# Attention scores of four graphs in one run on TensorE instead of two runs of two, in a two-layer graph attention kernel

## The chip, the cores and the metric

The kernel runs on one core of one Trainium2 chip. The metric is the device time in microseconds (us) of one execution, outputs compared with the reference. Before the change: 3203.19 us, median of three runs (3202.78 to 3203.3). Ratios are the mean time of one kernel's runs over that of the other's of the same rounds, so not quite the ratio of the medians that are quoted.

In the profile, PE is TensorE, PEld its weight loads, DVE is VectorE, ACT ScalarE, POOL GpSimd. A name like p1v is the PSUM bank p1 while it serves the matrix v; s is a bank of scores, av of the mix of values, e the exponentials, aT the normalised rows, transposed.

## The reference, cut to what matters

128 graphs of 128 nodes with 512 features, two layers, eight heads of 64, all in fp32. Layer 1 has an output matrix and a layer norm besides.

```python
scores = einsum('bihd,bjhd->bhij', Q, K) / sqrt(64)         # per graph and head: 128 x 128
scores = scores + (bias + log(adjacency + EPS))              # layer 1: log(clip(adj, 1e-8))
out    = einsum('bhij,bjhd->bihd', softmax(scores), V)
x      = out.reshape(...) + x                                # layer 0
x      = layer_norm(x + out.reshape(...) @ Wo.T + bo)        # layer 1
```

## The kernel before: what the change and the argument touch

Four graphs form a group; t counts the 64 groups of both layers (NG = 32, layer 1 from t = NG on). Each group has matrices v, q, k, and in layer 1 o. Each is a Strassen product P1 to P7 over seven slots; in many of them P2 (and P4 late on) is split again into four phases with small 128-column products. The functions of a slot are issued in program order on each engine.

```python
HALVES = slice(0, P // 2), slice(P // 2, P)

def matmul(dst, lhsT, rhs, start, stop):          # products: the array in two column halves
    for half in HALVES:
        nc.tensor.matmul(dst[half], lhsT[:, half], rhs, start=start, stop=stop, skip_group_check=True)

def scores(t, k):                                 # one visit: graphs 2k, 2k+1; the array in two row halves
    L, _ = split(t)
    s = {}
    for b in (2 * k, 2 * k + 1):
        s[b] = ps.tile([P, 2, KC, N], F32, tag="s", name=f"s_{t}_{b}", bufs=2)    # two banks a graph
        for c in range(KC):
            for r in range(2):
                ...
                nc.tensor.matmul(s[b][:, r, c], KT[t, k][at], QT[t, k][at], start=True, stop=True)
    for b, p in s.items():
        e = E[t, b] = work.tile([P, 2 * KC, N], F32, tag="e", name=f"e_{t}_{b}", bufs=2)
        nc.scalar.activation(e, p.rearrange("p r c j -> p (r c) j"), AF.Exp, scale=SCALE, ...)

def weigh(t, b):                                  # e *= adjacency, on VectorE
    ...
def mix(t, graphs):                               # e times V, again in column halves; its banks are "s" too
    ...
def move(t, k, engines):                          # 16 DMAs a pair: normalised rows to aT, in blocks of 32
    if k == 0:
        AT[t] = act.tile([P, G, KC, N], F32, tag="aT", name=f"aT_{t}")
    d = AT[t][:, 2 * k : 2 * k + 2].rearrange("p b c (t f) -> p (b c) t f", f=S)
    v = OR[t, k].rearrange("p b (c r) d -> p (b c) r d", r=2)
    for i in range(Q):
        for q in range(Q):
            src = v[i * S : (i + 1) * S, :, q // 2, (q % 2) * S : (q % 2 + 1) * S]
            engines[(i * Q + q) % len(engines)].dma_start(d[q * S : (q + 1) * S, :, i], src)
```

VectorE then transposes aT in place (turn) and the o matrix reads it. The eight PSUM banks are taken: four by the two buffers of s, and p0 to p3 by the products (p1 is P2's, p0 and p3 alternate from matrix to matrix). The two visits of a group stood at slots a + 4 and a + 11 (layer 1: a + 5 and a + 11), where a is the first slot behind k.

## Time and profile before

| | before |
|---|---|
| time, median | 3203.19 us |
| span of the profiled run | 3199.6 us |
| TensorE busy / share of the chain that ended last | 99% / 98% |
| VectorE, GpSimd, ScalarE busy | 68%, 63%, 33% |
| visits to the scores | 128 |
| TensorE's listed waits, all kinds | 8.5 us |

TensorE sets the time.

### The profile page before, as it was taken

The page shows a single profiled execution, that of the slowest core. Times are in us where ns is not written, and L with a number is a line of the kernel's source. Part 1 is how long each engine was busy: PE and PEld are TensorE (multiplying, and loading weights), DVE is VectorE, ACT ScalarE, POOL GpSimd, SP SyncE. Part 2 cuts the span into 40 slices and gives each one's busy share as a digit, 9 for nine tenths or more (in the row PEclk, how much of TensorE's full clock was granted, in tenths as well). Part 3 has the DMA queues.
Part 4 walks back from the last instruction along what each step waited for, and adds up shares of the span by engine and source line. Part 5 has one row for each costly group of instructions (what it writes and reads, how often), then busy time and mean ns, then how long its engine had stood idle before and what let it go on. Part 6 is the DMA issues. An engine that isn't in the chain of part 4 may idle for free.

```text
span 3199.6 us, 99332 instructions
## 1 busy us (share of the span) xinstructions
PE 3178.8 (99%) x41454; PEld 2454.4 (77%) x41454; DVE 2165.9 (68%) x4643; ACT 1043.3 (33%) x1763; POOL 2018.3 (63%) x2337
## 2 busy tenths in 40 slices
PE   9999999999999999999999999999999999999998
PEld 7777777777777777777887787878787777878785
DVE  6666666666666666676766666766666666766666
ACT  3333333333333333332323233323333233323332
POOL 4444433444433444468887878787787878787776
PEclk9999999999999999999999999999999999999999
DMA  5333333333333333342433434343433434343432
GB/s 126 84 80 82 79 80 75 84 81 82 79 75 80 84 81 81 94 110 54 82 87 76 95 73 98 68 95 72 83 85 76 94 74 97 72 100 65 92 77 77
DMA packets 1017266, 266.10 MB, mean 83 GB/s; under 512 B 942704, under 2 KB 949872, under 8 KB 1016816
## 3 DMA queue, kind: packets, MB, share of 16 engines
q1 hardware_dynamic: 1015152, 257.34, 36.2%
q8 instruction: 332, 5.44, 0.7%
q10 hardware_dynamic: 1408, 2.10, 0.2%
q14 instruction: 118, 0.97, 0.1%
q0 software_dynamic: 256, 0.26, 0.1%
HBM read 159.92 MB, written 67.11 MB: 71 GB/s over the span
## 4 chain that ended last, share of the span: by engine, by line
PE 98%; DVE 1%; POOL 0%; DMA 0%; issue 0%; ACT 0%; SPq 0%; DVEq 0%; POOLq 0%
PE p3v L135 10%; PE p3k L135 10%; PE p0q L135 10%; PE s L135 8%; PE av L135 7%; PE p2v L135 7%; PE p2q L135 7%; PE p2k L135 7%; PE p0o L135 7%; PE p0k L135 4%; PE p0v L135 4%; PE p3q L135 4%; PE p2o L135 3%; PE p1v L135 3%; PE p1k L135 3%; PE p1q L135 3%
## 5 line engine op out<-in xcount | busy, mean ns | idle before, releaser
L135 POOL TENSOR_TENSOR xn<-o,xn 128x512 f32<-128x512 f32 x128 | 149.0, 1186 | 653.6 <-DVE o L135 646.1
L135 DVE TENSOR_TENSOR e<-e,adjT 128x1024 f32<-128x1024 f32 x256 | 416.3, 1666 | 152.9 <-ACT e L135 152.9
L135 POOL TENSOR_TENSOR xn<-xn,row 128x512 f32<-128x512 f32 x256 | 356.3, 1414 | 128.6 <-DVE gw L135 120.5
L135 POOL TENSOR_TENSOR h<-h,xn 128x512 f32<-128x512 f32 x124 | 157.4, 1291 | 181.1 <-DVE h L135 181.1
L135 PE MATMUL av<-v,e 128*64 128x65 f32 x8192 | 262.4, 221 | 1.5 <-DVE e L135 1.5
L135 PE MATMUL s<-qT,kT 64*128 64x128 f32 x4096 | 263.1, 278 | 0.0
L135 PEld LDWEIGHTS av<-v,e 128*64 128x64 f32 x8192 | 258.0, 137 | 2.1 <-DVE e L135 2.1
L135 PEld LDWEIGHTS s<-qT,kT 64*128 64x128 f32 x4096 | 238.6, 188 | 22.2 <-issue 16.7
L135 PE MATMUL p3v<-wv,T 128*64 128x256 f32 (+1 forms) x2132 | 249.7, 361 | 2.5 <-DVE u3v L135 2.5
L135 PE MATMUL p3k<-T,wk 128*64 128x256 f32 (+1 forms) x2132 | 239.7, 360 | 0.0
L135 PE MATMUL p0q<-T,wq 128*64 128x256 f32 (+1 forms) x2132 | 239.7, 360 | 0.0
L135 ACT COPY o<-av 128x520 f32<-128x520 f32 x256 | 151.7, 593 | 168.1 <-PE av L135 159.3
L135 PEld LDWEIGHTS p3v<-wv,T 128*64 128x64 f32 x2132 | 163.3, 137 | 51.4 <-DVE u3v L135 2.9
L135 POOL TENSOR_TENSOR T<-xT 128x512 f32<-128x512 f32 x128 | 194.0, 1515 | 9.7 <-DVE xT L135 9.6
L135 DVE SCALAR_TENSOR_TENSOR gw<-xn,gw 128x512 f32<-128x512 f32 x256 | 196.5, 767 | 4.4
L135 POOL TENSOR_TENSOR h<-h,gamma 128x512 f32<-128x512 f32 x121 | 181.4, 1499 | 27.9 <-ACT h L135 27.9
L135 PEld LDWEIGHTS p3k<-T,wk 128*64 128x64 f32 x2132 | 149.0, 137 | 57.8
L135 PEld LDWEIGHTS p0q<-T,wq 128*64 128x64 f32 x2132 | 148.6, 137 | 58.1
L135 DVE STREAM_TRANSPOSE xT<-xT 128x512 f32<-128x512 f32 x252 | 176.9, 702 | 0.5 <-issue 0.5
L135 ACT ACTIVATE e<-s 128x1024 f32<-128x1024 f32 x128 | 124.3, 1023 | 124.9 <-PE s L135 124.9
L135 PE MATMUL p0o<-wo,T_o 128*64 128x256 f32 (+1 forms) x1368 | 161.1, 353 | 0.8 <-DVE u3o L135 0.4
L135 POOL TENSOR_TENSOR h<-h,beta 128x512 f32<-128x512 f32 x121 | 155.8, 1287 | 9.5
(271 smaller groups left out, 7146.0 us busy)
## 6 DMA issues: line engine op xcount, KB each, us to landing
x1d<-xn SPq DMA_DIRECT2D x64, 512.0 KB, 3.0
xT<-x1d SPq DMA_DIRECT2D x512, 64.0 KB, 2.5
xn<-x1d SPq DMA_DIRECT2D x64, 512.0 KB, 4.8
xT<-in_x_dram SPq DMA_DIRECT2D x496, 64.0 KB, 2.6
xn<-in_x_dram SPq DMA_DIRECT2D x62, 512.0 KB, 4.3
aT<-o SPq DMA_DIRECT2D x984, 32.0 KB, 2.0
out_dram<-h SPq DMA_DIRECT2D x60, 512.0 KB, 4.0
adjT<-in_adj_dram SPq DMA_DIRECT2D x256, 64.0 KB, 3.6
```

The source lines that it names most:

```text
L135: return lambda *args, **kw: self.tc.keep_in_program_order(f(*args, **kw))
```

## The change

Its intent is to cut the visits to the scores from two to one a group. The third graph has no s buffer, so it takes two banks of the products for a while (p1, and p0 or p3, whichever the matrix at hand doesn't use). As four graphs' exponentials now live at once, those of the first two go into buffers named h or xT. P2's phases, the weighings, moves, turns and row additions go to slots where those banks are free. In layer 1 from t > NG on, graphs 2,3 now come before 0,1. The core of the diff:

```diff
-    def scores(t, k):
+    def scores(t, graphs, spare=None):
...
-        for b in (2 * k, 2 * k + 1):
-            s[b] = ps.tile([P, 2, KC, N], F32, tag="s", name=f"s_{t}_{b}", bufs=2)
+        for i, b in enumerate(graphs):
+            k = b // 2
+            if i == 2:
+                s[b] = [ps.tile([P, KC, N], F32, tag=tag, name=f"s_{t}_{b}_{tag}") for tag in spare]
+            else:
+                p = ps.tile([P, 2, KC, N], F32, tag="s", name=f"s_{t}_{b}", bufs=2)
+                s[b] = [p[:, 0], p[:, 1], p]
...
+    EARLY = (0, 2, 3, 5)                    # slots of P2's four phases, now per matrix
+    for (which, t), n in at.items():
...
+        else:
+            phases = dict(v=(4, 5, 7, 9), q=(3, 4, 5, 7), k=(2, 3, 4, 5), o=(5, 7, 9, 10))[which]
...
-        step = 5 if t == NG else 7
-        for k in range(2 if t + 1 < LAST else 0):
-            put(pre, a + 4 + L * (1 - k) + step * k, scores, t, k)
...
+            visit, weighed, mixed, graphs = (
+                (3, (3, 3, 4, 5), (5, 7), (0, 1, 2, 3)), (3, (3, 3, 4, 5), (5, 7), (0, 1, 2, 3)), (5, (5, 5, 5, 7), (7, 9), (2, 3, 0, 1)),
+            )[(t >= NG) + (t > NG)]
+            put(pre, a + visit, scores, t, graphs, ("p1", "p0" if a // 7 % 2 else "p3"))
...
+                    put(post, m + (3, 1)[i], move, t, k, ...)
...
+                graphs = (2, 3, 0, 1) if t > NG else (0, 1, 2, 3)
+                put(post, first_pair, lambda t, bs: [turn(AT[t][:, b]) for b in bs], t, graphs[:2])
```

More of the change, by code (lines that the diff above doesn't have):

```diff
@@ L53 @@
     A11, A12, S4, NA22, S1, S2, S3 = range(7)
-    SLOTS = (
-        ("P1", "P4.1 b", "P2.1"), ("P4 b",), ("P3 b", "P4.2 b", "P2.2"), ("P6", "P4.3 b", "P2.3"), ("P5", "P4.4 b"),
-        ("P7", "P2.4"), (),
-    )
+    SLOTS = (("P1", "P4.1 b"), ("P4 b",), ("P3 b", "P4.2 b"), ("P6", "P4.3 b"), ("P5", "P4.4 b"), ("P7",), ())
     OPERANDS = {
@@ L169, in fast_path @@
     ps = ctx.enter_context(tc.tile_pool(name="ps", bufs=1, space=PSUM))
+    XTB = [act.tile([P, G, KC, N], F32, name=f"xT_{i}") for i in range(2)]
     X1D = [dram.tile([G, N, D], F32, name=f"x1d_{g}") for g in range(NG)]
@@ L184, in load_tiles @@
     def load_tiles(t):
-        XT[t] = act.tile([P, G, KC, N], F32, tag="xT", name=f"xT_{t}", bufs=2)
+        XT[t] = XTB[t % 2]
         AD[t] = act.tile([P, G, N], F32, tag="adjT", name=f"adjT_{t}", bufs=2)
@@ L343, in inner @@
             if phase == "1":
-                if i == "P2":
-                    out_tile()
                 t[i] = bank("p1") if i == "P2" else t["a"]
@@ L361, in inner @@
                 add(m, 0, p, v, 1, 3)
-                if i == "P2":
-                    add(1, 1, t["b"], t["u3"])
         def unit(i):
@@ L370, in unit @@
                 if (i, *phase) == ("P2", "1"):
-                    out_tile()
                     t["c"] = bank("p1")
@@ L377, in unit @@
                 return
+            if i == "C22":
+                return add(1, 1, t["b"], t["u3"])
             if i == "P1":
                 t["W"], t["B"] = W(), Bs()
+                out_tile()
                 t["a"] = bank("p3" if n % 2 else "p0")
@@ L390, in unit @@
                 kept("u3", p, 1, 1)
-                if "P2" not in inside:
-                    add(1, 1, t["b"], t["u3"])
             elif i == "P4":
@@ L458, in scores @@
                     at = half, c // 2, slice((c % 2 * 2 + b % 2) * N, (c % 2 * 2 + b % 2 + 1) * N)
-                    nc.tensor.matmul(s[b][:, r, c], KT[t, k][at], QT[t, k][at], start=True, stop=True)
-        for b, p in s.items():
-            e = E[t, b] = work.tile([P, 2 * KC, N], F32, tag="e", name=f"e_{t}_{b}", bufs=2)
-            nc.scalar.activation(
-                e, p.rearrange("p r c j -> p (r c) j"), AF.Exp, scale=SCALE,
-                **({"bias": C[t][:, 1, b : b + 1]} if L == 0 else {}),
-            )
+                    nc.tensor.matmul(s[b][r][:, c], KT[t, k][at], QT[t, k][at], start=True, stop=True)
+            if i > 1 or len(graphs) == 2:
+                E[t, b] = work.tile([P, 2 * KC, N], F32, tag="e", name=f"e_{t}_{b}", bufs=2)
+            elif t <= NG:
+                E[t, b] = work.tile([P, 2 * KC, N], F32, tag="h", name=f"e_{t}_{b}", bufs=2)
+            else:
+                E[t, b] = XT[t][:, 2 * i : 2 * i + 2].rearrange("p b c n -> p (b c) n")
+            e = E[t, b]
+            pieces = [(e[:, :KC], s[b][0]), (e[:, KC:], s[b][1])]
+            if i != 2:
+                pieces = [(e, s[b][2].rearrange("p r c j -> p (r c) j"))]
+            for e, p in pieces:
+                nc.scalar.activation(
+                    e, p, AF.Exp, scale=SCALE, **({"bias": C[t][:, 1, b : b + 1]} if L == 0 else {})
+                )
     def weigh(t, b):
@@ L494, in normalise @@
         o = OR[t, k]
-        if k == 0:
+        if t not in RC:
             RC[t] = small.tile([P, G, 2, KC], F32, tag="rc", name=f"rc_{t}", bufs=2)
@@ L527, in move @@
     def move(t, k, engines):
-        if k == 0:
+        if t not in AT:
             AT[t] = act.tile([P, G, KC, N], F32, tag="aT", name=f"aT_{t}")
@@ L674, in fast_path @@
             row_.append([(mats[j], i) for j, i in units if 0 <= j < len(mats)])
+    EARLY = (0, 2, 3, 5)
+    for (which, t), n in at.items():
+        if t < NG:
+            phases = EARLY if t == 0 else dict(v=(3, 4, 5, 7), q=(1, 2, 3, 5), k=EARLY)[which]
+        elif t == NG or (which, t) == ("v", NG + 1):
+            phases = dict(v=(3, 4, 5, 7), q=(1,), k=(0,), o=EARLY)[which]
+        elif (which, t) == ("o", LAST - 2):
+            phases = (3, 4, 5, 7)
+        else:
+            phases = dict(v=(4, 5, 7, 9), q=(3, 4, 5, 7), k=(2, 3, 4, 5), o=(5, 7, 9, 10))[which]
+        if (which, t) == ("o", NG):
+            phases = (0,)
+        for i, slot_ in enumerate(phases):
+            row_[7 * n + slot_].append((mats[n], f"P2.{i + 1}"))
+        row_[7 * n + 5].append((mats[n], "C22"))
     def slot(which, t, i):
@@ L689, in fast_path @@
         a = slot("k", t, 7)
-        step = 5 if t == NG else 7
-        for k in range(2 if t + 1 < LAST else 0):
-            put(pre, a + 4 + L * (1 - k) + step * k, scores, t, k)
-            for b in (2 * k, 2 * k + 1):
-                put(pre, a + 4 + L * (1 - k) + step * k, weigh, t, b)
-            if t + 1 < LAST:
-                m = a + 7 + L * (1 - k) + step * k
+        if t + 1 < LAST:
+            visit, weighed, mixed, graphs = (
+                (3, (3, 3, 4, 5), (5, 7), (0, 1, 2, 3)), (3, (3, 3, 4, 5), (5, 7), (0, 1, 2, 3)), (5, (5, 5, 5, 7), (7, 9), (2, 3, 0, 1)),
+            )[(t >= NG) + (t > NG)]
+            put(pre, a + visit, scores, t, graphs, ("p1", "p0" if a // 7 % 2 else "p3"))
+            for i, b in enumerate(graphs):
+                put(pre, a + weighed[i], weigh, t, b)
+            for i in range(2):
+                m, k = a + mixed[i], graphs[2 * i] // 2
                 put(pre, m, mix, t, (2 * k, 2 * k + 1))
-                put(post, m, normalise, t, k)
+                put(post, m + ((1, 4), (1, 0))[L][i], normalise, t, k)
                 if L == 1:
-                    put(post, m + 1, move, t, k, [nc.sync, nc.gpsimd] if t == NG and k else [nc.sync])
+                    put(post, m + (3, 1)[i], move, t, k, [nc.sync, nc.gpsimd] if t == NG and i else [nc.sync])
         if t + 1 < LAST:
-            put(post, a + 18, count, t)
+            put(post, a + 16, count, t)
         n, late = t + 1, int(t > NG)
@@ L708, in fast_path @@
                 put(post, first + (-1 if t == 0 else 2 + (8 if t > NG + 1 else 11) * (b // 2) * late), load_graph, n, b, nc.sync)
-                put(post, first + ((8, 9, 15, 17), (16, 17, 23, 24))[late][b], lambda n, b: turn(XT[n][:, b]), n, b)
+                put(post, first + ((8, 9, 16, 16), (19, 20, 23, 24))[late][b], lambda n, b: turn(XT[n][:, b]), n, b)
             put(post, first + (11, 16 if t == NG + 1 else 14)[late], load_adjacency, n, nc.sync)
-            put(post, first + (18, 26)[late], turn_adjacency, n)
+            put(post, first + (17, 31 if t > NG else 26)[late], turn_adjacency, n)
             put(post, first + (13, 17)[late], lambda n: TS.update({n: quarters(XT[n])}), n)
@@ L720, in fast_path @@
                 put(post, first + 17, load_natural, t + 1)
-            for k, i in enumerate((6, 6, 10, 10, 13, 13, 21, 21)):
+            for k, i in enumerate((1, 7, 10, 11, 13, 14, 18, 20)):
                 put(post, first + i, gate, t, k // 2, k % 2)
@@ L724, in fast_path @@
             for k in range(2):
-                put(post, first + (11, 22)[k], add_row, t, k)
+                put(post, first + (11, 25)[k], add_row, t, k)
         else:
@@ L728, in fast_path @@
             for k in range(2):
-                put(post, first + (27 if t == NG else 23) + (k if t in (NG, LAST - 1) else 10 * k), add_row, t, k)
+                put(post, first + ((27, 28) if t == NG else (28, 29) if t == LAST - 1 else (28, 32))[k], add_row, t, k)
             if n < LAST:
                 f = slot("v", n, 0)
-                turned = f + 18
-                put(post, f + (13 if t > NG else 17), lambda t: [turn(AT[t][:, b]) for b in (0, 1)], t)
-                put(post, f + (13 if t > NG else 17), lambda t: TO.update({t: quarters(AT[t])}), t)
-                if t > NG:
-                    put(post, f + 13, lambda t: inner_sums(TO[t], f"o{t}"), t)
-                put(post, turned, lambda t: [turn(AT[t][:, b]) for b in (2, 3)], t)
+                first_pair, turned = (f + 17, f + 18) if t == NG else (f + 15, f + 18)
+                graphs = (2, 3, 0, 1) if t > NG else (0, 1, 2, 3)
+                put(post, first_pair, lambda t, bs: [turn(AT[t][:, b]) for b in bs], t, graphs[:2])
+                put(post, first_pair, lambda t: TO.update({t: quarters(AT[t])}), t)
+                put(post, turned, lambda t, bs: [turn(AT[t][:, b]) for b in bs], t, graphs[2:])
                 for s in Strassen.SUMS:
@@ L740, in fast_path @@
                 if t > NG:
+                    put(post, turned, lambda t: inner_sums(TO[t], f"o{t}"), t)
                     put(post, turned, lambda t: inner_sums(TO[t], f"o{t}", "P4"), t)
@@ L743, in fast_path @@
                 for k in range(2):
-                    put(post, o + (2 + k if t == NG else 4 - 2 * k), residual, t, k)
+                    put(post, o + (2 + k if t == NG else ((4, 2) if t == LAST - 2 else (4, 5))[k]), residual, t, k)
                     if t == LAST - 2:
                         continue
-                    stat, scaled, end, stored = (((5, 6), 6, 9, 10), ((9, 10), 10, 14, 15))[k]
+                    stat, scaled, end, stored = (((5, 6), 8, 10, 10), ((9, 10), 10, 14, 16))[k]
                     for b in range(2):
@@ L791, in prepare @@
     def prepare():
-        last["o"] = act.tile([P, G, D], F32, tag="xT", name="o_last", bufs=2)
+        last["o"] = XTB[LAST % 2].rearrange("p b c n -> p b (c n)")
         AT[t] = act.tile([P, G, KC, N], F32, tag="aT", name="aT_last")
-        h = act.tile([P, G, D], F32, tag="xT", name="h_last", bufs=2)
+        h = XTB[(LAST + 1) % 2].rearrange("p b c n -> p b (c n)")
         HS[t, 0], HS[t, 1] = h[:, 0:2], h[:, 2:4]
@@ L849, in fast_path @@
     for i, f, *of in (
-        (5, scores, t, 0), (5, weigh, t, 0), (5, weigh, t, 1), (8, mix, t, (0, 1)), (9, normalise_one, 0),
-        (9, normalise_one, 1), (9, scores, t, 1), (9, weigh, t, 2), (9, weigh, t, 3), (10, transpose_one, 0),
+        (5, scores, t, (0, 1)), (5, weigh, t, 0), (5, weigh, t, 1), (8, mix, t, (0, 1)), (9, normalise_one, 0),
+        (9, normalise_one, 1), (9, scores, t, (2, 3)), (9, weigh, t, 2), (9, weigh, t, 3), (10, transpose_one, 0),
         (10, transpose_one, 1), (11, stats, u, 2), (11, stats, u, 3), (11, root, u, slice(2, 4)),
```

## The prediction

> **What bounds the kernel now.** I read the page first (busy time, chain), then the list of waits of TensorE alone, then the timeline around one visit to the scores, because the change is about how those visits lie on TensorE. From the page:
>
> ```profile
> span 3199.6 us, 99332 instructions
> PE 3178.8 (99%) x41454; PEld 2454.4 (77%) x41454; DVE 2165.9 (68%) x4643; ACT 1043.3 (33%) x1763; POOL 2018.3 (63%) x2337
> PE 98%; DVE 1%; POOL 0%; DMA 0%; issue 0%; ACT 0%; SPq 0%; DVEq 0%; POOLq 0%
> ```
>
> TensorE is busy for 99% and carries 98% of the chain that ended last. The first lines of its waits, longest first in total:
>
> ```profile
> PE p3v L135 <- DVE u3v L135: 2.5, 1, 2.5
> PE av L135 <- DVE e L135: 1.5, 2, 1.1
> ```
>
> The nine kinds of wait listed there add up to 8.5 us in the whole span. So hardly any time can be won by removing a wait; the time can only fall if TensorE's own instructions take less, and it rises by whatever new waits appear. No instruction of TensorE is taken out by the diff, so what is left is how the instructions follow each other. One visit to the scores (two graphs, 32 instructions, as each fp32 matmul shows as two) in the timeline, in layer 0; columns are start and length in us:
>
> ```profile
> 807.85 0.39 PE L135 MATMUL p1q<-innerP,wq0i 128*64 128x128 f32 x4
> ...
> 808.07 1.90 PE L135 MATMUL p3q<-T,wq 128*64 128x256 f32 x16
> ...
> 809.79 0.39 PE L135 MATMUL p1q<-innerP,wq 128*64 128x128 f32 x4
> ...
> 810.11 1.86 PEld L135 LDWEIGHTS s<-qT,kT 64*128 64x128 f32 x32 [0.17 <-PE p3q L135]
> 810.11 2.06 PE L135 MATMUL s<-qT,kT 64*128 64x128 f32 x32
> ...
> 811.32 2.12 ACT L135 ACTIVATE e<-s,c 128x1024 f32<-128x1024 f32 x2 [0.68 <-PE s L135]
> ...
> 812.09 1.49 PEld L135 LDWEIGHTS p2q<-T,wq 128*64 128x64 f32 x16
> 812.10 1.95 PE L135 MATMUL p2q<-T,wq 128*64 128x256 f32 x16
> ...
> 813.87 0.39 PE L135 MATMUL p3q<-T,wq 128*64 128x256 f32 x2
> ```
>
> Read the starts. Four p1q matmuls take 0.22 us until a product follows (807.85 to 808.07), but 0.32 us until scores follow (809.79 to 810.11): 0.10 more, and the weight load of the first score starts only with its matmul. A product of 16 takes 1.72 (808.07 to 809.79), the one after the scores 1.77 (812.10 to 813.87): 0.05 more. Inside the visit, two narrow windows of the same timeline, each showing what of the scores was running there (up to the visit's last pair in both):
>
> ```profile
> 810.77 1.40 PE L135 MATMUL s<-qT,kT 64*128 64x128 f32 x22
> ```
>
> ```profile
> 811.66 0.50 PE L135 MATMUL s<-qT,kT 64*128 64x128 f32 x6
> ```
>
> So 16 instructions, eight pairs, start in 811.66 - 810.77 = 0.89 us: 0.111 a pair. The visit's 16 pairs should take 1.78; it takes 812.10 - 810.11 = 1.99, 0.21 more, split between the first pair and the step out. The scores' form is 64*128 (64 rows, all columns), that of products and mixes 128*64: the array is halved the other way. All together a visit costs 0.10 + 0.21 + 0.05 = 0.36 us; with the rounding of two decimals, 0.35 is as good. It is hidden in "busy", because ends of matmuls are modelled.
>
> **What the Trainium skill says.** "TensorEngine Tiling (Array Packing)", Key Properties: a change of the tiling mode, not of the tile alone, drains TensorE. The trace agrees in kind: 0.35 us a visit as above, and none between products and mixes, which have the same halving (0.22 after four p1 matmuls in both cases). "TensorE: Matmul & The Clock Gate", Part 2, step 1: weight loads are pulled ahead of running matmuls while they don't conflict. The trace shows that they are not at the switch (load and matmul of the first score both at 810.11). The Tiling page, Gotcha 1: row tiles running together must write different PSUM banks; so each graph's scores take two banks, which is why the third graph needs two borrowed ones: four banks are the two "s" buffers, four are p0 to p3. "PSUM — Partial Sum Buffer", bank collisions: engines are to be kept apart by bank, which is why each reuse of a bank here is a semaphore wait that could stall TensorE. The trace of before shows hardly any.
>
> **The change part by part.** (1) Visits. 4096 score instructions at 32 a visit are 128 visits: two for each of 64 group-layers. After it, 63 of them have one visit of 64 instructions, and the last keeps its two: 65. Removed: 63 x 0.35 = 22.0 us, all on the path, as TensorE is the path.
> (2) The mixes stay two per group, and have the products' mode: nothing.
> (3) The P2 phases are moved, not changed: 0.22 us for four instructions wherever they stand. Nothing, if their operands are ready.
> (4) The third graph's exponential becomes two ScalarE instructions of 512 columns. One of 1024 is 1.114 us in layer 0; two copies of 512 (0.59 each on the page's neighbours, row by form) suggest about 1.2. Some 0.1 us x 63 on an engine that is 33% busy: off the path.
> (5) New buffers (E in "h" or in xT) cost no instruction. The transposes, gates, sums and moves go to other slots: the same work on engines at 68% and 63%.
> (6) New waits. Let T be the start of a run. Its length is 32 x 0.111 + 0.21 = 3.77 us. The first exponential starts at T + 1.21 (810.11 to 811.32) and ends at T + 2.33 in layer 0, T + 2.24 in layer 1 (1.024 us each there). The fourth graph reuses the first one's buffer at T + 0.10 + 24 x 0.111 = T + 2.77: 0.4 us spare. What ScalarE had before (the copy of P4 in layer 0, of P6 in layer 1) is a whole slot old by then. The third exponential leaves the borrowed p1 by about T + 3.9 and the other bank by T + 4.5; the next P2 phase on p1 comes after a product, at T + 3.77 + 1.77 = T + 5.5. Spare 1 us and more.
> VectorE's weighing (mean 1.76 us in layer 0, 1.58 in layer 1, 2.29 in the slowest) starts after the first exponential. Layer 0: first mix at about T + 5.5 + 0.65 + 1.73 + 0.22 = T + 8.1; two weighings end by T + 6, at worst T + 7. No wait. Layer 1 is tighter: only P7 and one phase stand between, first mix at T + 6.2, its second graph at T + 7.1; two weighings end at T + 5.5 on the mean, T + 6.9 at worst. The second mix wants the fourth graph's by T + 11.6; three weighings, 1.3 us of additions and the fourth end at T + 9.9 on the mean and T + 12.8 when all four are slow. So a wait of about 1 us in a few of the 31 groups: I allow 2 us in all.
> Sum: 3203.2 - 22.0 + 2 = 3183 us.
>
> **The rivals.** (a) The buffers bind: TensorE waits in the run for the fourth graph's buffer, or at the first mix for VectorE, which is now held by up to three weighings in a row. If each run lost 0.5 us, 32 us would be added: 3213. For it: the list of all waits has VectorE waiting for exponentials 125 times, 152.9 us in all, and it is a queue in order, so products' additions stand behind. Against it: the margins worked out above, and that the phases were moved exactly so that p1 is free and the additions aren't needed at once. (b) The row switch is not per visit but partly per graph (a change of banks costs it as well); then less than 22 us comes back. Against it: in the old visit of two graphs, the pitch is 0.111 across the change of graph. (c) Layer 1's transfers: both moves of the normalised rows to aT now go out in one slot, 32 issues; if the second pair is late, the transposes hold VectorE and then TensorE. Before, the last of them was issued at a similar time and turned in the same slot, and VectorE waited 2.0 us in all for aT. Some groups losing 1 us would make it 3190 to 3200. (d) The moved work removes waits as well: at most the 8.5 us there are, most of them in the first and last 40 us or at the change of layers: 3178.
>
> **Range and chances.** The switch is measured to about 0.03 us a visit, which is 2 us in the sum; the waits are one-sided, 0 to some 10 us. So 3183, from 3177 to 3193. 2% is 64 us. For a gain of that size there is nothing on TensorE to take away; for such a loss each run would have to lose over 1.3 us. Faster 0.01, same 0.97, slower 0.02.
>
> **What would show it.** In the profile after: 41454 matmuls still, TensorE at 99%; runs of 64 scores that take about 3.77 us to the next product; one slow first pair per run; the scores' share of the chain down; ScalarE's exponentials in three forms. TensorE's waits should stay under some 12 us in all. Wrong would be: a wait of TensorE on ScalarE's e inside the runs, or on VectorE's e before the mixes, some 63 times; or a pitch of the scores that breaks at every graph; or a span that falls by much less though no such wait shows.

## The result, and the profile after

3170.97 us, median of four runs (3170.23 to 3172.1), beside 3202.99 (3202.66 to 3203.3). The ratio is 0.99, 95% interval 0.9883 to 0.9918. That is a gain of 32 us, within 2% as forecast, but below the range of 3177 to 3193. From the page of the changed kernel:

```profile
span 3168.5 us, 98958 instructions
PE 3149.2 (99%) x41454; PEld 2474.2 (78%) x41454; DVE 2216.4 (70%) x4643; ACT 1044.1 (33%) x1826; POOL 2116.2 (67%) x2337
```

The same 41454 matmuls as before, in 31.1 us less span. The longest two of TensorE's waits there (total, times, longest):

```profile
PE p1v L132 <- DVE xT L132: 1.9, 1, 1.9
PE p1o L132 <- DVE h L132: 1.3, 1, 1.3
```

Both are single events, the first at the start, the second near the end. None is in a run of scores. The waits for u3v (2.5 us) and e (1.5 us) that before had at the change of layers are gone. One run of layer 1 in the timeline of the changed kernel (s_p is the third graph in the borrowed banks):

```profile
2029.33 2.06 PE L132 MATMUL s<-qT,kT 64*128 64x128 f32 x32
2031.21 1.06 PE L132 MATMUL s_p<-qT,kT 64*128 64x128 f32 x16
2032.11 1.06 PE L132 MATMUL s<-qT,kT 64*128 64x128 f32 x16
2033.10 1.95 PE L132 MATMUL p0o<-wo,T_o 128*64 128x256 f32 x16
2034.88 0.61 PE L132 MATMUL p1o<-wo,aT 128*64 128x128 f32 x8
```

The run takes 2033.10 - 2029.33 = 3.77 us, as worked out before; the next product 1.78. There are 63 such runs, and the last group's two visits. And of what uses the borrowed banks, in layer 0 (count, then shortest, median and longest in ns):

```profile
L132 ACT ACTIVATE e<-s_p,c x64: 686/693/699, 51.9 to 1395.5; 128x512 f32<-128x512 f32 x64
```

Two of these are 1.39 us where one of 1024 columns was 1.114: 0.27 us more, not the 0.1 that I had estimated, but on an engine with room.

To see where the time went I measured in both traces the distance from q's first product to that of the next group, the same place of the program each time:

| median of a group | before | after | less |
|---|---|---|---|
| layer 0 | 43.716 us | 43.324 us | 0.39 us |
| layer 1 | 55.122 us | 54.561 us | 0.56 us |

A visit saved should be 0.35. Layer 0 gives 0.04 more, layer 1 0.21 more. So something else in layer 1 got cheaper, and no list of waits had shown it.

**Where it was hidden.** In the timeline of the kernel before, behind the second mix of a group in layer 1:

```profile
2500.81 2.04 PE L135 MATMUL av<-v,e 128*64 128x65 f32 x64
2502.68 2.00 PE L135 MATMUL p2o<-wo,aT 128*64 128x256 f32 x15
2504.41 0.38 PE L135 MATMUL p0o<-woi,innerP_o 128*64 128x128 f32 x2
2504.52 0.38 PE L135 MATMUL p2o<-wo,aT 128*64 128x256 f32 x1
...
2507.43 2.06 PE L135 MATMUL s<-qT,kT 64*128 64x128 f32 x32
```

A product should be one row of x16. Here its last matmul starts after the next product has begun (2504.52 behind 2504.41): the two column halves of the array no longer run together. The trace's records of TensorE's queue there tell why (start in us; "asks" is an instruction of the sequencer that only waits for semaphores, S100, 102 and 104 to 109 being those of the DMA queue):

```
2502.114 asks S106 S105      2502.562 asks S106            2502.677 p2o matmul, first half
2502.224 asks S107 S104      2502.623 load p2o (S101)      2502.894 p2o matmul, first half
2502.330 asks S108 S102      2502.668 asks S107 S105       2502.955 load p2o (S100)
2502.436 asks S109 S100      2502.774 asks S108 S104       2502.986 p2o matmul, second half
                             2502.879 asks S109 S102
```

P3 of the o matrix is the first to read aT's graphs 2,3. They came in 16 DMAs over eight semaphores, the first eight for one half's columns, the last eight for the other's. So TensorE asks for all eight, then for all eight again. Everything had landed long before (VectorE had turned these graphs by 2483.68), yet each asking instruction starts 0.105 us or more behind the last. During the mix the asking starts 0.51 us before the first load (2502.114 to 2502.623), enough for one round and not for two, and the second half starts at 2502.986, 0.31 us behind the first. Over all 31 groups the halves' first loads at P3 are 0.334 us apart in the median. TensorE counts as busy all the while, since the first half works. The lag stays until the scores, which need both halves. The Trainium skill has the two ends of this: "TensorEngine Tiling (Array Packing)", Key Properties, says that tiles run independently, and "Perfetto Trace Analysis", Identifying Dependency Chains, that such instructions may be put in front of one that waits for several engines. The trace agrees with both (most of the waits here are on DMA semaphores) and adds the price.

My theory after reading: before, P1 asked for the pair moved first, P3 for the pair moved second, behind a mix. At P1 the two rounds were hidden: in the group looked at they started 1.60 us before the load (2482.236 to 2483.840), and the halves load 0.007 us apart. In the changed kernel graphs 2,3 are moved first and 0,1 last. P1 reads 0,1, and as a semaphore only counts up, its asking covers the earlier moves as well; P3 need not ask. Its trace agrees: no asking for the moves' semaphores stands before P3's first loads, and its row is whole:

```profile
2041.87 1.90 PE L132 MATMUL p2o<-wo,aT 128*64 128x256 f32 x16
```

A lag is left at P1 itself:

```profile
2020.35 0.39 PE L132 MATMUL p1k<-xT,wk1i 128*64 128x128 f32 x4
2020.56 1.91 PE L132 MATMUL p0o<-wo,aT 128*64 128x256 f32 x15
2022.29 0.27 PE L132 MATMUL p3k<-T,wk 128*64 128x128 f32 x1
2022.31 0.38 PE L132 MATMUL p0o<-wo,aT 128*64 128x256 f32 x1
```

Again x15 and a straggler, but there the halves are 0.2 us apart at the start (0.14 us of a group's time, as will be seen). One thing is new there: the last ask of the first round also waits for VectorE's turn of the pair moved last. It lasts 0.34 us in each of 30 groups (0.05 is the usual) and ends 0.034 us behind the rise of VectorE's semaphore; only then comes the second round. The list of waits does not show it, as matmuls run on meanwhile. Asking instructions in the whole trace: 1549 before, 1133 after.

### The profile page after: what moved, and what is told of

The parts are those of the page before. It is cut to its first block, busy times and chain, and to the rows that moved or that the text cites.

```text
span 3168.5 us, 98958 instructions
## 1 busy us (share of the span) xinstructions
PE 3149.2 (99%) x41454; PEld 2474.2 (78%) x41454; DVE 2216.4 (70%) x4643; ACT 1044.1 (33%) x1826; POOL 2116.2 (67%) x2337
## 4 chain that ended last, share of the span: by engine, by line
PE 98%; DVE 1%; DMA 0%; POOL 0%; ACT 0%; issue 0%; SPq 0%; POOLq 0%; ACTq 0%; DVEq 0%
PE p3v L132 10%; PE p0q L132 10%; PE p3k L132 10%; PE av L132 7%; PE p2k L132 7%; PE p2q L132 7%; PE p2v L132 7%; PE p0o L132 7%; PE s L132 6%; PE p0v L132 4%; PE p3q L132 4%; PE p0k L132 4%; PE p2o L132 3%; PE p1k L132 3%; PE p1q L132 3%; PE p1v L132 3%
## 5 line engine op out<-in xcount | busy, mean ns | idle before, releaser
L132 POOL TENSOR_TENSOR xn<-o,xn 128x512 f32<-128x512 f32 x128 | 171.9, 1364 | 691.9 <-DVE o L132 691.9
L132 DVE TENSOR_TENSOR e<-e,adjT 128x1024 f32<-128x1024 f32 x196 | 272.8, 1406 | 47.2 <-ACT e L132 47.2
L132 DVE SCALAR_TENSOR_TENSOR gw<-xn,gw 128x512 f32<-128x512 f32 x256 | 284.8, 1113 | 1.1
L132 PE MATMUL s<-qT,kT 64*128 64x128 f32 x3088 | 200.4, 276 | 0.0
L132 PE MATMUL av<-v,e 128*64 128x65 f32 x6272 | 199.7, 221 | 0.0
L132 PEld LDWEIGHTS s<-qT,kT 64*128 64x128 f32 x3088 | 182.7, 188 | 18.1 <-issue 18.0
L132 PEld LDWEIGHTS av<-v,e 128*64 128x64 f32 x6272 | 196.6, 137 | 0.1
L132 DVE TENSOR_TENSOR t1v<-p1v,t1v 128x128 f32<-128x128 f32 x189 | 54.8, 290 | 182.4 <-PE p1v L132 182.3
L132 POOL TENSOR_TENSOR h<-h,gamma 128x512 f32<-128x512 f32 x121 | 154.8, 1279 | 32.7 <-ACT h L132 30.4
L132 DVE TENSOR_TENSOR xT<-xT,adjT 128x1024 f32<-128x1024 f32 x60 | 128.1, 2174 | 52.0 <-ACT xT L132 52.0
```

The lines of the kernel that those rows point to most:

```text
L132: return lambda *args, **kw: self.tc.keep_in_program_order(f(*args, **kw))
```

## The experiments

Eleven kernels; the kernel before: 3202.83, 3201.53, 3202.36 and 3202.98 us. The changed kernel was not run again, so differences from it of less than about 1.5 us say nothing. All were correct. Group times are the medians as above.

**e1: the run cut in two.** This undoes the saved visit; besides, in layer 1 the third graph's weighing is issued behind its scores.

```diff
-            put(pre, a + visit, scores, t, graphs, spare)
+            put(pre, a + visit, scores, t, graphs, spare, 0)     # the first two graphs
+            put(mid, a + visit, scores, t, graphs, spare, 1)     # the last two, behind the slot's first product
```

> The changed kernel with its run of four graphs cut in two, the first product of the slot (P6 in layer 0, P7 in layer 1) between the pairs; banks, buffers and all other slots stay. If each visit costs TensorE 0.35 us for the two switches of the array's halving, 63 more visits give 63 x 0.35 = 22 us: 3171 + 22 = 3193 us (up to 2 more as two graphs are weighed later). If most of the gain came from the other slots, it stays between 3171 and 3180.

3193.64 us (3192.34 to 3194.2), against 3170.97 for the changed kernel. The span is 3190.6, 22.1 us more than after; a group of layer 0 takes 43.673, 0.349 more. In its timeline:

```profile
2044.10 2.06 PE L132 MATMUL s<-qT,kT 64*128 64x128 f32 x32
2046.09 1.95 PE L132 MATMUL p0o<-wo,T_o 128*64 128x256 f32 x16
2047.96 1.16 PE L132 MATMUL s_p<-qT,kT 64*128 64x128 f32 x16
2048.96 1.06 PE L132 MATMUL s<-qT,kT 64*128 64x128 f32 x16
```

The product between takes 1.87 instead of 1.73: 0.05 behind one switch and 0.10 ahead of the next. The first theory stands, with its size: 63 x 0.35.

**e2: the moves in the old order**, graphs 0,1 first, in the changed kernel.

```diff
-                    put(post, m + (3, 1)[i], move, t, k, ...)
+                    put(post, m + (3, 1)[i], move, t, k if t == NG else 1 - k, ...)
-                graphs = (2, 3, 0, 1) if t > NG else (0, 1, 2, 3)
+                graphs = (0, 1, 2, 3)
```

> The changed kernel with layer 1's moves to aT, and the turns after them, in the order of before (graphs 0,1 first, then 2,3). Theory: layer 1's extra 0.18 us a group comes from how often TensorE must ask the DMA queues' semaphores before it first reads aT; with graphs 2,3 moved last, P1 asks for the first pair and P3, right behind a mix, again for the second. Then semaphore instructions on TensorE rise by some 100 to 200 and the time by 0.1 to 0.3 us x 30 groups: 3174 to 3180 us. Rival: the extra has nothing to do with it (the visits' order or P2's phases): 3171, within 1.

3176.31 us (3175.19 to 3177.44). Asking instructions 1343, 210 more. All of it is in layer 1's groups, about 0.19 us each; layer 0 is the same to the hundredth. That is most of the 0.21 in question. P3 behind the mix has its straggler back:

```profile
2043.55 2.06 PE L132 MATMUL p2o<-wo,aT 128*64 128x256 f32 x15
2045.28 0.38 PE L132 MATMUL p0o<-woi,innerP_o 128*64 128x128 f32 x2
2045.45 0.38 PE L132 MATMUL p2o<-wo,aT 128*64 128x256 f32 x1
```

As the theory has it; the halves' first loads are 0.334 us apart there again.

**e3: the new order alone, in the kernel before.**

```diff
-        for k in range(2 if t + 1 < LAST else 0):
+        for j in range(2 if t + 1 < LAST else 0):
+            k = 1 - j if t > NG else j
...
-                    put(post, f + 13, lambda t: inner_sums(TO[t], f"o{t}"), t)
+                    put(post, turned, lambda t: inner_sums(TO[t], f"o{t}"), t)      # now behind the second pair's turn
```

> The kernel before with one thing of the change alone: in layer 1 graphs 2,3 are visited, moved and turned first, then 0,1. Two visits stay, as do all of P2's phases. Theory of the semaphores: P1 then asks for everything, P3 behind the mix for nothing, the half of the array no longer lags by 0.3 us in each group: 3203 - 30 x 0.2 = 3197 us (0.1 to 0.3 a group: 3194 to 3200). Rival: 3203, within 1, or slower, as the inner sums come later.

3208.76 us (3207.69 to 3209.81): slower, a miss for the theory, as its rival allowed. The asking at P3 is gone (1223 instructions instead of 1549), but a wait has taken its place:

```profile
PE p1v L135 <- DVE h L135: 11.0, 29, 0.7
```

0.38 us in each group. VectorE's two weighings took 4.31 us instead of 3.69. I put that down to GpSimd's work, pushed back by the inner sums, more of which now runs beside them; that was not tested alone. The additions to h behind them come late, and P2 of v waits for their bank. So e3 neither shows nor refutes the theory: two things changed.

**e4: no borrowed banks.** The third graph takes an s buffer like the others.

```diff
-            if i == 2:
-                s[b] = [ps.tile([P, KC, N], F32, tag=tag, ...) for tag in spare]
+            if i == 9:      # never
```

> The changed kernel without borrowed banks: the third graph takes the next of the two score buffers, as the fourth does. If the borrowed banks are what makes the run possible, TensorE waits for ScalarE in each run: the third graph is due 1.9 us after the run's start, the first exponential ends at 2.3 to 2.4; the fourth waits another 0.1. 0.55 to 0.65 us x 63 = 35 to 41 us: 3206 to 3212 us, no better than before. Rival: a pause inside the run is partly hidden by queued weight loads: 3171 to 3190.

3208.48 us (3208.07 to 3209.72), 37.5 more than the changed kernel and slower than before. Its waits:

```profile
PE s L132 <- ACT e L132: 10.5, 33, 0.3
PE s L132 <- ACT xT L132: 6.9, 30, 0.3
```

The list gives 17.4 us, half of the loss: 0.70 us a group in layer 0 and 0.52 in layer 1, from the distances, 0.3 and 0.2 of it listed. Here a wait inside the run thus costs about twice what the list shows; what fills the rest I did not take apart. The borrowed banks are what makes one run pay.

**e5: the tail.** The last o matrix but one with its phases at slots 0, 2, 3, 5 (`phases = EARLY` instead of `(3, 4, 5, 7)`).

> The changed kernel with the phases of the last output matrix but one (layer 1, the one that ends beside the last group) back at slots 0, 2, 3, 5. Its trace shows TensorE waiting 1.33 us for VectorE's h in the tail, which before did not have. If that is why the tail got 2.6 us longer, it falls by 1.3 to 2.6 us: 3168.5 to 3169.7. Rival: the tail is set by what follows (the last group's own chain), then 3171, within 0.5.

3171.81 us (3170.86 to 3172.97): no gain. The wait for h is gone, another is there, on GpSimd's inner sums that aren't ready so early:

```profile
PE p1o L132 <- POOL innerP_o L132: 2.7, 1, 2.7
```

**e6: k's last phase behind the next matrix's first product**, in layer 1 (`k=(2, 3, 4, 7)` instead of `k=(2, 3, 4, 5)`), to give the sequencer a lead before o's P1.

> The changed kernel with the fourth phase of P2 of layer 1's k moved behind the first product of the next matrix (slot 5 to slot 7). The output matrix's first product, where TensorE asks for aT's DMA semaphores, then follows a long product instead of short phases, so the sequencer has a lead. Theory: the lag of one half (0.14 us a group in the trace) goes: 3171 - 30 x 0.14 = 3167. Rival: the lag stays, as the asking itself takes the time: 3171, within 1.

3183.43 us (3183.26 to 3183.69), 12 us slower: a miss.

```profile
2023.23 1.90 PE L132 MATMUL p3k<-T,wk 128*64 128x256 f32 x16
2025.07 2.14 PE L132 MATMUL p0o<-wo,aT 128*64 128x256 f32 x15
```

The product p3k takes 1.84 to the next one, not 1.73. The last ask of the first round, which waits for VectorE's turn, lasts 1.51 us here (0.34 in the changed kernel): VectorE's semaphore rises at 2024.982, the ask ends at 2025.017, p0o's first load starts at 2025.042, and the second round of asking runs from 2025.092 (first matmuls of p0o at 2025.073, 2025.311 and, in the second half, 2025.516). In the changed kernel the phase between p3k and P1, 0.43 us long, had covered most of that wait. There was less lead, not more: the halves' first loads are 0.443 us apart instead of 0.201, and a group took 0.43 us longer.

**e7: the change of layers.** In the kernel before, the output rows' weightings, four VectorE instructions in 4.30 us that stood in front of a weighing in the chain of waits, two slots later (`(12, 12, 15, 15)` for `(10, 10, 13, 13)`).

> The kernel before with the four weightings of the output's rows at the change of layers two slots later (12, 12, 15, 15 instead of 10, 10, 13, 13), so that they don't stand in VectorE's queue before the second pair's weighing. Theory: TensorE's wait of 1.5 us for VectorE's e there (1.1 and 0.4) goes: 3203 - 1.5 = 3201.5. Rival: something else takes its place: 3203.

3203.82 us (3203.61 to 3204.42): no gain. The waits for e are gone from the list, and

```profile
PE pbo L135 <- DVE gw L135: 3.5, 1, 3.5
```

is there: the bias product needs those rows. The queue of VectorE was the cause, but this place for them isn't free.

**e8: e3 with GpSimd's row additions four slots later** (first + 27 and 33 for first + 23 and 33), to let its sums run earlier.

> The kernel before with layer 1's order reversed as in e3, and the two row additions of GpSimd in layer 1 four slots later, so that GpSimd's sums don't slow VectorE's weighing as they did there. In e3 the lag at P3 was gone but TensorE waited 0.38 us in each group for VectorE's h. Theory: without that wait the semaphores' gain is left, 3202.5 - 30 x 0.2 = 3196.5 us (3194 to 3199), and TensorE's waits for h are gone. Rival: the order itself costs, 3203 or more.

3210.46 us (3209.4 to 3210.63): a miss again.

```profile
PE p1v L135 <- DVE h L135: 12.5, 26, 0.6
```

The sums did move, but the later of them took 2.26 us each beside the weighings, which now took 4.42 us. This shift did not remove the wait.

**e9: fewer semaphores, same order.** In the changed kernel only the two loops of the moves are exchanged. DMAs go to the eight semaphores in turn, so with i inside, the eight moves that fill one half's columns hit four semaphores twice, instead of eight once.

```diff
-        for i in range(Q):
-            for q in range(Q):
+        for q in range(Q):
+            for i in range(Q):
                 src = v[i * S : (i + 1) * S, :, q // 2, (q % 2) * S : (q % 2 + 1) * S]
-                engines[(i * Q + q) % len(engines)].dma_start(d[q * S : (q + 1) * S, :, i], src)
+                engines[(q * Q + i) % len(engines)].dma_start(d[q * S : (q + 1) * S, :, i], src)
```

> The changed kernel with the two loops around the moves to aT exchanged, the same 32 moves per group: moves that touch the same columns then share four of the eight semaphores of the queue, so the first half of the array has four to ask for before P1 of the output matrix and the second half the other four, instead of all eight at the first. Theory: the lag of one half there (0.14 us a group) shrinks: 3171 - 30 x 0.1 = 3168 us. Rival: the number asked in all counts, not how they are spread, or the moves land later: 3171, within 1.

3166.48 us (3166.14 to 3168.64), 4.5 less than the changed kernel. 1010 asking instructions; a group of layer 1 takes 54.425, 0.136 less, layer 0 the same. At P1 of o:

```profile
2019.81 1.90 PE L132 MATMUL p0o<-wo,aT 128*64 128x256 f32 x16
2021.53 0.61 PE L132 MATMUL p3k<-T,wk 128*64 128x128 f32 x8
```

Whole rows: the straggler is gone, and the halves' first loads are 0.010 us apart instead of 0.201.

**e10: e9 with the last o matrix but one at slots 2, 3, 4, 7.**

> As e9, and the last output matrix but one has its phases in slots 2, 3, 4, 7: the third phase's addition then stands before the last group's weighing in VectorE's queue, and the first comes late enough for GpSimd's inner sums, which e5 ran into. Theory: the wait of 1.33 us for h in the tail goes: 1 to 2 us less than e9, 3166 to 3167 us. Rival: another wait takes its place, as in e5: the same as e9 within 0.5.

3165.29 us (3164.95 to 3165.97), the best here; ratio to before 0.9885, interval 0.9868 to 0.9901. The wait for h is gone, 0.9 us for the inner sums came. Against e9 the span is 0.9 us shorter, 0.6 of it in the tail. The times of the two just fail to overlap (e9 from 3166.14, e10 up to 3165.97); executions of one kernel differ by up to 3 us here, so I don't call the gain shown.

**e11: the exchanged loops in the kernel before**, the same edit as e9's, nothing of the change.

> The kernel before with the two loops around the moves to aT exchanged as in e9, nothing else: no order, slot or bank of the change. If layer 1's groups of before lost time because TensorE asks for eight semaphores of the queue at P3 behind a mix (a lag of 0.3 us of one half in the trace), asking for four at each half takes most of it away: 3202.4 - 30 x 0.2 = 3196.5 us (0.1 to 0.3 a group: 3193.5 to 3199.5), and the interleaved matmuls behind P3 are gone from its timeline. Rival: e3 and e8 were slower because the asking doesn't matter in before: 3202.4 within 1.

3192.16 us (3190.95 to 3192.84), ratio to before 0.9968, interval 0.9956 to 0.998. Its timeline behind the mix:

```profile
2496.72 2.04 PE L135 MATMUL av<-v,e 128*64 128x65 f32 x64
2498.59 1.90 PE L135 MATMUL p2o<-wo,aT 128*64 128x256 f32 x16
...
2503.01 1.16 PE L135 MATMUL s<-qT,kT 64*128 64x128 f32 x16
```

From p2o to the scores 4.42 us; in the kernel before 2507.43 - 2502.68 = 4.75. The 0.33 us had been there in each group of layer 1, and exchanging two loops takes it away without any of the change. With that, layer 1's group times close:

| layer 1, a group | two visits | one run | less |
|---|---|---|---|
| moves as they were | 55.122 | 54.561 | 0.561 |
| loops exchanged | 54.769 | 54.425 | 0.344 |
| less | 0.353 | 0.136 | |

With the asking out of the way the run alone is worth 0.344, the predicted 0.35. The other 0.217 of the change in layer 1 are the asking: its lag cost 0.353 before and 0.136 after.

## Why the prediction was wrong

- **What bounds it: right.** TensorE stayed at 99%, and the time fell by what its instructions took less.
- **Part 1, the visits: right, with its size.** 22.0 us predicted; e1 gives 22.1 of span, e9 against e11 0.344 a group.
- **Parts 2 and 4, mixes and exponentials: right in effect.** The split exponential cost 0.27 us more, not 0.1, and nothing waited for it.
- **Part 6, new waits: 2 us allowed, 0.2 came in the list** (one event, at a mix at the change of layers). The margins held; e4 shows what they are worth. Unlisted came the sequencer's 0.34 us for VectorE's turn ahead of P1, in 30 groups. As I read the traces, it starts the second round of asking late; that lag cost the 0.136 us a group that e9 takes away.
- **The failed step is the reading of the list of waits as all that TensorE loses**: "hardly any time can be won by removing a wait", and from it rival (d), "the 8.5 us there are", which set the low end of the range. (Its sum is off as well: 8.5 us less than 3181 is 3172.7, and 3178 allows for only 3 of them. The result lies below both.) The list counts idle time of the whole engine. Nearly 0.35 us in each of layer 1's groups was lost by one column half alone, some 10 us in all (e11: 10.8), and the changed order of the moves removed more than half of it by the way: 0.217 us a group, of which e2 gives back 0.19. Part 5 had called the moves "the same work on engines at 68% and 63%"; their order acted on TensorE.
- **A second miss in (d)**: part of the 8.5 us listed did go. At the change of layers the kernel gained about 4.9 us beyond the visits, 4.0 of them the two waits (p3v and av), each behind a pair's two weighings on VectorE. e7 shows that VectorE's queue held av there; which of the moved parts ended both waits I did not separate. The start and the tail lost 3.0 us, also not foreseen; the start's 0.4 is within what the runs' first q products differ by (18.8 to 19.6 us).

The sum of the span, in us:

| term | predicted | measured | from |
|---|---|---|---|
| 63 visits | 22.0 | 22.0 | 63 x 0.349, e1 |
| layer 1's groups beyond that | 0 | 5.8 | 29 distances of 0.548 on the mean, less 0.349 each |
| layer 0's groups beyond that | 0 | 1.4 | 32 distances, 0.044 each |
| change of layers | 0 | 4.9 | the rest: the two distances there, less two visits |
| start and tail | 0 | -3.0 | 0.4 and 2.6 longer |
| new waits | -2 | in the above | |
| sum | 20 | 31.1 | spans 3199.6 and 3168.5 |

Open: layer 0's 0.04 us. In the trace of before one of its two mixes takes 1.905 us instead of 1.868, in that of after both take 1.868; I did not test why. Rival (b), a cost per bank, did not show: the run's pitch is the same across its four graphs. Nor did (c), the transfers: VectorE's idle time before its 124 turns of aT is 3.5 us in all, 2.0 before.

## What to carry to other kernels

A run of matmuls that halves the array the other way costs a fixed price at its two ends, here 0.35 us, so gather such runs, and borrow PSUM banks for it if the next user of the bank comes a product later. Where an array works in halves, an engine that is busy for 99% can still lose time: look in the timeline for rows that should be whole and come as x15 and x1, and at the semaphore instructions ahead of them, how many they are and how long they last. Here a tile filled by many DMAs was asked for semaphore by semaphore by its first reader, however long ago it had landed; issue the DMAs so that one reader needs few semaphores, and let the first reader be one that also covers the earlier moves.

## What the Trainium skill lacked or had wrong

- "TensorEngine Tiling (Array Packing)", Key Properties, says that a change of mode drains, not what it costs: 0.10 us ahead of the first matmul, 0.10 at the second pair, 0.10 and 0.05 on the way back, 0.35 us for a visit (e1: 22.1 us for 63).
- The same place says that tiles run independently, not that one half may lag the other through several products: 0.31 us at the start in the trace of before, carried 4.75 us on to the next change of mode. A matmul of the next product started at 2504.405, ahead of the last of the product before it at 2504.519.
- "Perfetto Trace Analysis", Identifying Dependency Chains, names the inserted semaphore instructions but not their price: up to two semaphores each, 0.105 us from one to the next, even when all have long been reached. Eight semaphore waits ahead of the tile's reader instead of sixteen saved 10.8 us of this kernel (e11).
- No page that I read says that the order in which a tile's DMAs are issued sets how many semaphores its first reader asks for: 1549 instructions against 1306 by exchanging two loops.
